# A graph attention stack on one core: the last all-node block of layers 2 and 3 holds three row tiles, and row tile 24 is gathered

## The chip, the core and the metric

The kernel runs on one core of a Trainium2 chip. The metric is device time in microseconds of that core, from start to end of one execution. A profiled execution gives the trace; the timed runs are separate executions without a profile.

## The reference

Four graph attention layers work on the same 4096 nodes with 256 features each. `adj` is a 4096 x 4096 0/1 matrix with a density of about 1/256 and ones on the diagonal. Each layer computes attention weights between every node and its neighbours, a softmax over the neighbours, the weighted sum of the projected neighbours, a residual and a layer norm:

```python
e = leaky_relu(s1[:, None] + s2[None, :], 0.2)        # per head
att = softmax(where(adj > 0, e, -huge), axis=1)
x = layernorm(x + att @ h)                            # h = x @ W, per head
```

Layers 0 and 1 have four heads of 64, layer 2 has two heads of 128. Layer 3 has one head of 256, computes the softmax of e and of -e, passes both weighted sums through one matrix and an ELU, and then does the same residual and norm.

## The kernel before, in words

Nodes are cut into 32 tiles of 128. A layer has two ways to compute a row tile (128 output nodes).

**Gathered.** Because the graph is sparse, layer 0 also builds lists of the neighbours of each row tile. `RowTile.load` (L781) fetches their projected values from HBM: one plain load of the tile's own rows and 13 indirect transfers `G<-vals,idx` of 128 rows each (L797), issued by POOL one after another. They come in two halves of seven places: half 0 has six gathers and reads only nodes of tiles under `MIX` = 23 (L85, L798); half 1 has seven and may read any node. `RowTile.half` (L835) then computes weights on ScalarE (`w`, L907 in layer 2, L874 in layer 3), masks them on VectorE (L909, L876, L878) and multiplies on TensorE (L928). The mask bits are spread to bytes at L660. The buffers `G` are four slots per half; a half takes one slot in layer 2 and two in layer 3, so in layer 3 POOL can be two tiles ahead.

**All-node.** `whole_rows` (L1168) computes a block of four row tiles against all 32 node tiles, without gathers. One unit is one node tile j: SyncE loads `vw` (L1188), VectorE spreads mask bits (L660), ScalarE computes weights `pw` for 512 columns (L1200, or L1203 with L1205 or L1207), VectorE masks them (L1201 or L1208), TensorE does four matmuls for each head (L1211). Layer 2's units do both heads (32 units a block); layer 3's do one of its two sums (64 units a block). All TensorE inputs are fp32; the trace has two records for each matmul. `WHOLE` (L115) names the blocks of each layer: block 7 in layer 1, blocks 3, 7, 6 in layer 2, blocks 7, 6 in layer 3. `ORDER` (L117) is the rest, in rising order: layer 2 gathers 20 tiles (0 to 11, 16 to 23), layer 3 gathers 24 (0 to 23).

**Order of the work.** Each engine runs its instructions in the order in which the program was built. `half_with_whole` (L1046) is one half step: the half of a gathered tile, the projection of a finished tile into the next layer's values (transposes L677, copy L682, matmuls L691, exponent L711, product L725, store `vals<-row` L728), then the norm of the gathered tile before (L1360), then some units. `whole` (L995) paces the units evenly, so that they are used up six half steps before the layer's end; the block's tiles are finished after that (in layer 3 one per half step, through `zw`, L1376). A finished tile is projected two half steps later, tiles under `MIX` first (L1051). In `close` (L1106) what is left is projected, and the next layer's first loads and ten units are put in (`AHEAD`). Layer norms are done in groups of tiles (`GROUPS`, L82)[...].

So layer 3's first gathers on POOL wait for the values of all tiles under 23, and its half-1 gathers for all 32. POOL issues in program order: all of layer 2's gathers come before layer 3's first.

Of the kernel before, what the change touches and what calls it, by code (L numbers as in the profile page):

```python
# [37 lines left out]
F32 = mybir.dt.float32  # L38
# [3 lines left out]
I32 = mybir.dt.int32  # L42
I8 = mybir.dt.int8
U8 = mybir.dt.uint8
AF = mybir.ActivationFunctionType
# [5 lines left out]
P = 128  # L51
N = 4096
F = 256
NT = N // P
KT = F // P
BT = 4
# [22 lines left out]
UNITS = (1 + FIRST, NPACK - FIRST)  # L79
FULL = ((0,), tuple(range(NPAIR - FIRST, NPACK - FIRST)))  # L80
PAIRS = (tuple(range(1, 1 + FIRST)), tuple(range(NPAIR - FIRST)))
GROUPS = (((24, 4),), ((24, 2), (28, 1), (31, 2)), ((16, 2), (17, 1), (20, 2), (24, 1), (31, 2)), ((24, 1), (31, 4)))  # L82
LEAD = 4
LATE = 4
MIX = 23  # L85
# [26 lines left out]

WHOLE = ((), (7,), (3, 7, 6), (7, 6))  # L115
AHEAD = 10
ORDER = tuple([m for m in range(NT) if m // BT not in w] for w in WHOLE)  # L117

LEAST = 2.0611536224385579e-09

# [63 lines left out]
class Program:  # L184
# [99 lines left out]
    def lists(self, ctx):  # L284


        tc, nc, ins, shared = self.tc, self.nc, self.ins, self.shared
# [91 lines left out]
        class Block:  # L379
# [21 lines left out]
            def squeeze(self, part):  # L401
                js = slice(part * JG, (part + 1) * JG)
                src = self.mk.rearrange("p j t c -> p (j t c)").bitcast(I32) \
                    .rearrange("p (j t c) -> p j t c", j=JG, t=BT)
                w = P // 4
                for k in (4, 2, 1):
                    w //= 2
                    dst = self.bits[:, js] if k == 1 else wk.tile([P, JG, BT, w], I32, name=f"fold{k}", bufs=1)
                    nc.vector.scalar_tensor_tensor(dst, src[:, :, :, w:], k, src[:, :, :, :w],
                                                   op0=ALU.logical_shift_left, op1=ALU.bitwise_or)  # L410
                    src = dst
                if part == BT - 1:
                    rows = shared["v"][0][self.blk % 2][:N, :BW].rearrange("(j p) w -> p j w", p=P)
                    nc.sync.dma_start(out=rows, in_=self.bits.rearrange("p j t w -> p j (t w)").bitcast(F32))
                    if any(self.blk in w for w in WHOLE):
                        nc.sync.dma_start(out=shared["bitsW"][self.blk], in_=self.bits)

            def sort(self):
# [111 lines left out]
        prog, blocks = self, {}  # L530
# [424 lines left out]
class Layer:  # L955
# [212 lines left out]
    def whole_rows(self):  # L1168
        n, nc, prog, sh = self.n, self.nc, self.prog, self.shared
        H, Wd, T = HEADS[n], WIDTH[n], TERMS[n]  # L1170
        groups = [range(H)] if n < 3 else [(0,), (1,)]
        for blk in WHOLE[n]:
            tiles = range(blk * BT, (blk + 1) * BT)
            S = prog.bk.tile([P, T, BT, P], F32, name="Sw")
            for it, m in enumerate(tiles):
                nc.sync.dma_start(out=S[:, :, it, :], in_=sh["e"][n][m].partition_broadcast(P))
            bits = self.block_bits(blk)
            zs = [None] * BT
            for heads in groups:
                accs = [prog.bank(prog.pfour) for _ in range(BT)]  # L1180
                c0, c1 = heads[0] * Wd, (heads[-1] + 1) * Wd
                vs = {}

                def fetch(j):
                    if j >= NT:
                        return
                    vs[j] = prog.vp.tile([P, c1 - c0], F32, name="vw")
                    nc.sync.dma_start(out=vs[j], in_=sh["v"][n][0][j * P:(j + 1) * P, c0:c1])  # L1188

                for j in range(4):  # L1190
                    fetch(j)
                for j in range(NT):
                    fetch(j + 4)
                    mj = self.bytes(bits, j)
                    v = vs.pop(j)
                    for h in heads:
                        p = prog.dp.tile([P, BT, P], F32, name="pw")
                        d = sh["d"][n][:, j, h if n < 3 else 0:h + 1 if n < 3 else 1]
                        if n < 3:
                            nc.scalar.activation(p, S[:, h], AF.Exp, bias=d)  # L1200
                            nc.vector.scalar_tensor_tensor(p, p, LEAST, mj, op0=ALU.max, op1=ALU.mult)  # L1201
                        else:
                            nc.scalar.activation(p, S[:, 0], AF.Relu, bias=d)  # L1203
                            if h == 0:
                                nc.scalar.activation(p, p, AF.Exp, bias=sh["shift2"])  # L1205
                            else:
                                nc.scalar.activation(p, p, AF.Exp, scale=-1.0)  # L1207
                            nc.vector.tensor_tensor(p, p, mj, op=ALU.mult)  # L1208
                        c = h * Wd - c0
                        for it in range(BT):  # L1210
                            nc.tensor.matmul(accs[it][:, c:c + Wd], p[:, it, :], v[:, c:c + Wd],  # L1211
                                             start=(j == 0 and h == heads[0]), stop=(j == NT - 1),
                                             skip_group_check=True)
# [12 lines left out]

    def whole_heads(self):
# [7 lines left out]
        for blk in WHOLE[n]:  # L1235
            tiles = range(blk * BT, (blk + 1) * BT)
            S = prog.bk.tile([P, T, BT, P], F32, name="Sw")
# [10 lines left out]
            bits = self.block_bits(blk)  # L1248
            z = prog.bk.tile([P, BT, H, Wd], F32, name="zh")
            for up, flat in TWOS:  # L1250
                bu, bf = prog.bank(prog.pwhole), prog.bank(prog.pwhole)
                vs = {}
# [9 lines left out]
                for j in range(NT):  # L1262
                    fetch(j + 4)
                    mj = self.bytes(bits, j)
                    v = vs.pop(j)
                    p = {}
                    for h in (up, flat):
                        p[h] = prog.dp.tile([P, BT, P], F32, name="pw")
                        nc.vector.scalar_tensor_tensor(p[h], S[:, h], c[:, j, h:h + 1], mj, op0=ALU.max, op1=ALU.mult)  # L1269
                    how = dict(stop=j == NT - 1, skip_group_check=True)  # L1270
                    for it in range(BT):
# [5 lines left out]
                nc.scalar.copy(z[:, :, up, :], bu[:, :BT * Wd].rearrange("p (t c) -> p t c", t=BT))  # L1277
                turned = prog.bk.tile([Wd, BT, P], F32, name="turned")
                nc.scalar.copy(turned, bf[:Wd, :].rearrange("p (t i) -> p t i", t=BT))
                self.set_banks()  # L1280
                bt = prog.bank(prog.banks)
                for it in range(BT):
                    nc.tensor.transpose(bt[:, it * Wd:(it + 1) * Wd], turned[:, it, :], sh["ident"][:Wd, :Wd])
                nc.scalar.copy(z[:, :, flat, :], bt[:, :BT * Wd].rearrange("p (t c) -> p t c", t=BT))
# [12 lines left out]

    def load_x(self, m):
        y = self.prog.ld.tile([P, F], F32, name="y", bufs=13)
# [545 lines left out]
```

## Time and profile before

| what | value |
|---|---|
| median of 3 timed runs | 2787.8 us (2785.93 to 2805.77) |
| the profiled execution's own time | 2012.93 us |
| its span | 2011.1 us |
| TensorE clock granted, mean | 0.936 |
| PE, PEld, DVE, ACT, POOL busy | 1796.4, 1481.6, 1551.8, 1498.1, 1391.5 us |
| HBM traffic over the span | 224 GB/s |
| gathers `G<-vals,idx` | 1352, of 1025 ns mean |
| L1200 and L1203, 512 columns | 711 and 709 ns |
| L1201 and L1208, 512 columns | 686 and 689 ns |
| L909, 512 and 640 columns | 684 and 817 ns |
| L877, 512 and 640 columns | 715 and 821 ns |

The timed runs are 775 us longer than the profiled execution. All durations here are from that execution. Layer 2's last gather starts at 1489.8 us after the span's start, layer 3's first at 1533.2 and its last at 1978.4.

PE's busy time is modelled and its single durations overlap. What a matmul costs is better read from the chain of waits, where runs of records of one line stand with the time they took together. A gap of 0.3 us named "issue" stands between one gather and the next on POOL.

### The profile page before, as it was taken

How to read it: one execution, taken by the hardware profiler on the slowest of the kernel's cores; microseconds unless marked ns; L12 is line 12 of the kernel's file. 1: busy time of each engine (PE TensorE's matmuls, PEld its weight loads, DVE VectorE, ACT ScalarE, POOL GpSimd, SP SyncE). 2: the span in 40 equal slices, each digit the busy share in tenths (PEclk: the TensorE clock that was granted, in tenths of full speed). 3: DMA queues.
4: the chain of work that ended last, by engine and by line, in shares of the span. 5: the costliest groups of instructions: out<-in, count | busy, mean ns of one | idle time of the engine just before them, and what ended most of it. 6: DMA issues, size and time to landing. Idle time of an engine off the chain costs nothing.

```text
span 2011.1 us, 46792 instructions
## 1 busy us (share of the span) xinstructions
PE 1796.4 (89%) x15281; PEld 1481.6 (74%) x15281; DVE 1551.8 (77%) x5095; ACT 1498.1 (74%) x4659; POOL 1391.5 (69%) x1387
## 2 busy tenths in 40 slices
PE   5758889988999699998998989999998899899995
PEld 3537777777778589887886788898886677577773
DVE  3458988888889599988887877888876576676765
ACT  4559999898878577877666788877774687676863
POOL 0067777777777777777777677777753777767772
PEclk7758999999899799999999999999999999999998
DMA  8799999989767766666656656667666888888883
GB/s 292 227 336 325 319 298 286 293 293 296 217 170 203 200 177 190 180 182 178 179 167 183 194 158 189 199 189 203 184 187 188 248 266 247 266 251 251 258 250 105
DMA packets 291947, 453.59 MB, mean 226 GB/s; under 512 B 90246, under 2 KB 206059, under 8 KB 291692
## 3 DMA queue, kind: packets, MB, share of 16 engines
q0 software_dynamic: 74880, 227.83, 38.7%
q1 hardware_dynamic: 212194, 218.46, 35.0%
q10 hardware_dynamic: 4618, 4.20, 0.6%
q8 instruction: 123, 2.02, 0.4%
q14 instruction: 132, 1.08, 0.2%
HBM read 401.51 MB, written 48.81 MB: 224 GB/s over the span
## 4 chain that ended last, share of the span: by engine, by line
PE 46%; DMA 14%; ACT 12%; POOL 10%; DVE 9%; issue 6%; SPq 1%; DVEq 0%; ACTq 0%; POOLq 0%
PE bank L928 22%; PE bank L1211 12%; POOL G L797 10%; DMA G<-vals,idx 8%; ACT w L907 7%; PE bank L691 5%; DVE w L864 3%; DMA raw<-in_adjB_dram 2%; PE bank L1274 2%; ACT mk L399 1%; ACT pw L1200 1%; PE bank L1272 1%; DMA G<-vals 1%; PE bank L522 1%; PE bank L524 1%
## 5 line engine op out<-in xcount | busy, mean ns | idle before, releaser
L797 POOL DMA_INDIRECT G<-vals,idx x1352 | 1386.0, 1025 | 587.9 <-issue 350.0
L928 PE MATMUL bank<-G,w 128*64 128x130 f32 (+5 forms) x9156 | 920.8, 304 | 72.7 <-DVE w L864 60.7
L907 ACT ACTIVATE w<-S,G 128x64 f32<-128x64 f32 (+1 forms) x3080 | 824.3, 351 | 125.3 <-DMA G<-vals,idx 116.2
L928 PEld LDWEIGHTS bank<-G,w 128*64 128x64 f32 (+1 forms) x9156 | 741.4, 156 | 232.1 <-DVE w L864 76.5
L1211 PE MATMUL bank<-vw,pw 128*128 128x129 f32 (+1 forms) x2560 | 419.4, 322 | 13.7 <-issue 6.3
L1211 PEld LDWEIGHTS bank<-vw,pw 128*128 128x128 f32 x2560 | 375.1, 194 | 53.8 <-issue 17.7
L864 DVE SCALAR_TENSOR_TENSOR w<-w,bank 128x1024 f32<-128x1024 f32 (+1 forms) x240 | 322.7, 1345 | 10.2 <-ACT w L907 8.7
L691 PE MATMUL bank<-wext,xT 128*128 128x268 f32 (+3 forms) x640 | 185.6, 424 | 16.2 <-ACT xT L682 14.9
L874 ACT ACTIVATE w<-S,G 128x64 f32<-128x64 f32 (+1 forms) x329 | 104.1, 352 | 72.1 <-DMA G<-vals,idx 48.7
L691 PEld LDWEIGHTS bank<-wext,xT 128*128 128x128 f32 x640 | 121.4, 207 | 40.8 <-ACT xT L682 17.7
L1200 ACT ACTIVATE pw<-Sw,d 128x512 f32<-128x512 f32 x192 | 134.3, 711 | 21.0 <-PE bank L1211 12.5
L1201 DVE SCALAR_TENSOR_TENSOR pw<-pw,mw 128x512 f32<-128x512 f32 x192 | 129.5, 686 | 26.2 <-ACT pw L1200 25.1
L399 ACT ACTIVATE mk<-raw 128x1024 uint8<-128x1024 int32 x128 | 129.6, 1049 | 21.1 <-DMA raw<-in_adjB_dram 21.0
L1208 DVE TENSOR_TENSOR pw<-pw,mw 128x512 f32<-128x512 f32 x128 | 87.9, 689 | 63.1 <-ACT pw L1205 38.3
L903 DVE TENSOR_TENSOR w<-S,G 128x384 f32<-128x384 f32 x180 | 91.1, 509 | 41.8 <-DMA G<-vals,idx 36.2
L1203 ACT ACTIVATE pw<-Sw,d 128x512 f32<-128x512 f32 x128 | 89.7, 709 | 27.2 <-PE bank L928 10.4
L1272 PE MATMUL bank<-vw,pw 128*128 128x65 f32 x512 | 89.7, 258 | 17.5 <-DVE pw L1269 17.5
L1274 PE MATMUL bank<-pw,vw 128*65 128x128 f32 x512 | 99.7, 278 | 0.0
L1272 PEld LDWEIGHTS bank<-vw,pw 128*128 128x128 f32 x512 | 78.7, 195 | 26.2 <-issue 24.8
L1269 DVE SCALAR_TENSOR_TENSOR pw<-Sw,cw,mw 128x512 f32<-128x512 f32 x128 | 92.8, 740 | 0.0
L682 ACT COPY xT<-bank 128x256 f32<-128x256 f32 x128 | 45.7, 359 | 58.2 <-PE bank L677 37.9
L660 DVE TENSOR_TENSOR mw<-bw,pat 128x128 int32<-128x128 int32 x288 | 80.6, 285 | 1.6
(197 smaller groups left out, 1893.6 us busy)
## 6 DMA issues: line engine op xcount, KB each, us to landing
raw<-in_adjB_dram SPq DMA_DIRECT2D x128, 512.0 KB
G<-vals,idx POOLq DMA_INDIRECT x1352
vw<-vals SPq DMA_DIRECT2D x128, 128.5 KB
S<-edge SPq DMA_DIRECT2D x60, 256.0 KB
vw<-vals SPq DMA_DIRECT2D x96, 129.0 KB
xp<-y SPq DMA_DIRECT2D x96, 128.0 KB
y<-xp SPq DMA_DIRECT2D x96, 128.0 KB
vals<-row SPq DMA_DIRECT2D x64, 152.0 KB
```

What stands on the lines that cost most here:

```text
L399: nc.scalar.activation(self.mk[:, 2 * q:2 * q + 2], src, AF.Copy)
L691: nc.tensor.matmul(pp[:, :c1 - c0], self.xT[:, k, :], wext[:, k, c0:c1], start=(k == 0), stop=(k == KT - 1 and brow is None))
L797: nc.gpsimd.indirect_dma_start(out=self.row(half, k), out_offset=None, in_=self.values[:N + 1 if half else MIX * P, :].rearrange("r (k c) ...
L864: return nc.vector.scalar_tensor_tensor(pair, pair, LEAST, mh2, op0=ALU.max, op1=ALU.mult)
L874: nc.scalar.activation(w[0][:, u, rows], S[:, 0, rows], AF.Relu, bias=d(g, 0))
L907: nc.scalar.activation(w[h][:, u, rows], S[:, h, rows], AF.Exp, bias=d(g, h))
L928: nc.tensor.matmul(a, w[h][:, u, rows], b, start=half == 0 and u == 0 and (n == 3 or h == turns[0][0]), stop=half == 1, skip_group_check=True)
L1200: nc.scalar.activation(p, S[:, h], AF.Exp, bias=d)
L1201: nc.vector.scalar_tensor_tensor(p, p, LEAST, mj, op0=ALU.max, op1=ALU.mult)
L1211: nc.tensor.matmul(accs[it][:, c:c + Wd], p[:, it, :], v[:, c:c + Wd], start=(j == 0 and h == heads[0]), stop=(j == NT - 1), skip_group_ch ...
L1272: nc.tensor.matmul(bu[:, it * Wd:(it + 1) * Wd], p[up][:, it, :], v[:, up * Wd:(up + 1) * Wd], start=j == 0 and it == 0, **how)
L1274: nc.tensor.matmul(bf[:Wd, it * P:(it + 1) * P], v[:, flat * Wd:(flat + 1) * Wd], p[flat][:, it, :], start=j == 0 and it == 0, **how)
```

## The change

A block of `WHOLE` is now a range of row tiles that may be shorter than four. The last block of layers 2 and 3 becomes tiles 25 to 27 in place of 24 to 27. Tile 24 joins the gathered tiles as the last of `ORDER` (21 in layer 2, 25 in layer 3). The block's weights, masks and products are computed for three tiles: 384 columns in place of 512, three matmuls in place of four. Node values are loaded as before. The groups of norms follow. Layer 1's block 7 is the same as before. The diff, without layer 1's function and other places where only a 4 becomes a `g`:

```diff
-GROUPS = (((24, 4),), ((24, 2), (28, 1), (31, 2)), ((16, 2), (17, 1), (20, 2), (24, 1), (31, 2)), ((24, 1), (31, 4)))
+GROUPS = (((24, 4),), ((24, 2), (28, 1), (31, 2)), ((16, 2), (17, 1), (20, 2), (25, 1), (31, 2)), ((25, 1), (28, 3), (31, 4)))

...
-WHOLE = ((), (7,), (3, 7, 6), (7, 6))
+WHOLE = (
+    (),
+    (range(28, 32),),
+    (range(12, 16), range(28, 32), range(25, 28),),
+    (range(28, 32), range(25, 28),),
+)
-ORDER = tuple([m for m in range(NT) if m // BT not in w] for w in WHOLE)
+ORDER = tuple([m for m in range(NT) if not any(m in g for g in w)] for w in WHOLE)

...
         groups = [range(H)] if n < 3 else [(0,), (1,)]
-        for blk in WHOLE[n]:
-            tiles = range(blk * BT, (blk + 1) * BT)
+        for tiles in WHOLE[n]:
+            g = len(tiles)
             S = prog.bk.tile([P, T, BT, P], F32, name="Sw")
             for it, m in enumerate(tiles):
                 nc.sync.dma_start(out=S[:, :, it, :], in_=sh["e"][n][m].partition_broadcast(P))
-            bits = self.block_bits(blk)
-            zs = [None] * BT
+            bits = self.block_bits(tiles)
+            zs = [None] * g
             for heads in groups:
-                accs = [prog.bank(prog.pfour) for _ in range(BT)]
+                accs = [prog.bank(prog.pfour) for _ in range(g)]
                 c0, c1 = heads[0] * Wd, (heads[-1] + 1) * Wd
                 vs = {}
...
                     for h in heads:
-                        p = prog.dp.tile([P, BT, P], F32, name="pw")
+                        p = prog.dp.tile([P, BT, P], F32, name="pw")[:, :g]
                         d = sh["d"][n][:, j, h if n < 3 else 0:h + 1 if n < 3 else 1]
                         if n < 3:
-                            nc.scalar.activation(p, S[:, h], AF.Exp, bias=d)
+                            nc.scalar.activation(p, S[:, h, :g], AF.Exp, bias=d)
                             nc.vector.scalar_tensor_tensor(p, p, LEAST, mj, op0=ALU.max, op1=ALU.mult)
                         else:
-                            nc.scalar.activation(p, S[:, 0], AF.Relu, bias=d)
+                            nc.scalar.activation(p, S[:, 0, :g], AF.Relu, bias=d)
                             if h == 0:
                                 nc.scalar.activation(p, p, AF.Exp, bias=sh["shift2"])
                             else:
                                 nc.scalar.activation(p, p, AF.Exp, scale=-1.0)
                             nc.vector.tensor_tensor(p, p, mj, op=ALU.mult)
                         c = h * Wd - c0
-                        for it in range(BT):
+                        for it in range(g):
                             nc.tensor.matmul(accs[it][:, c:c + Wd], p[:, it, :], v[:, c:c + Wd],
                                              start=(j == 0 and h == heads[0]), stop=(j == NT - 1),
                                              skip_group_check=True)
                     if n == 3 and heads[0] == 0 and j == NT - 1:
                         def between(accs=accs):
-                            for it in range(BT):
+                            for it in range(g):
                                 zs[it], last = self.positive(accs[it], whole=True)
                             return last
                         self.between = between
...
-    def block_bits(self, blk):
+    def block_bits(self, tiles):
+        blk, t = divmod(tiles[0], BT)
         bits = self.prog.mwp.tile([P, NT, BT, MW], I32, name="bw")
         self.nc.sync.dma_start(out=bits, in_=self.shared["bitsW"][blk])
-        return bits
+        return bits[:, :, t:t + len(tiles)]
     def bytes(self, bits, j):
-        mj = self.prog.mup.tile([P, BT, P // 4], I32, name="mw")
+        g = bits.shape[2]
+        mj = self.prog.mup.tile([P, BT, P // 4], I32, name="mw")[:, :g]
         spread(self.nc, mj, bits[:, j], self.shared["pat"])
-        return mj.rearrange("p t i -> p (t i)").bitcast(U8).rearrange("p (t i) -> p t i", t=BT)
+        return mj.rearrange("p t i -> p (t i)").bitcast(U8).rearrange("p (t i) -> p t i", t=g)
```

More of the change, by code (lines that the diff above doesn't have):

```diff
@@ L414, in squeeze @@
                     nc.sync.dma_start(out=rows, in_=self.bits.rearrange("p j t w -> p j (t w)").bitcast(F32))
-                    if any(self.blk in w for w in WHOLE):
+                    if any(g[0] // BT == self.blk for w in WHOLE for g in w):
                         nc.sync.dma_start(out=shared["bitsW"][self.blk], in_=self.bits)
@@ L1234, in whole_heads @@
         nc.vector.tensor_scalar(c, c, HUGE, TINY, op0=ALU.min, op1=ALU.max)
-        for blk in WHOLE[n]:
-            tiles = range(blk * BT, (blk + 1) * BT)
-            S = prog.bk.tile([P, T, BT, P], F32, name="Sw")
+        for tiles in WHOLE[n]:
+            g = len(tiles)
+            S = prog.bk.tile([P, T, BT, P], F32, name="Sw")[:, :, :g]
             for it, m in enumerate(tiles):
@@ L1247, in whole_heads @@
                 nc.vector.tensor_scalar(S[:, h], S[:, h], LEAST, HUGE, op0=ALU.mult, op1=ALU.min)
-            bits = self.block_bits(blk)
-            z = prog.bk.tile([P, BT, H, Wd], F32, name="zh")
+            bits = self.block_bits(tiles)
+            z = prog.bk.tile([P, BT, H, Wd], F32, name="zh")[:, :g]
             for up, flat in TWOS:
@@ L1267, in whole_heads @@
                     for h in (up, flat):
-                        p[h] = prog.dp.tile([P, BT, P], F32, name="pw")
+                        p[h] = prog.dp.tile([P, BT, P], F32, name="pw")[:, :g]
                         nc.vector.scalar_tensor_tensor(p[h], S[:, h], c[:, j, h:h + 1], mj, op0=ALU.max, op1=ALU.mult)
                     how = dict(stop=j == NT - 1, skip_group_check=True)
-                    for it in range(BT):
+                    for it in range(g):
                         nc.tensor.matmul(bu[:, it * Wd:(it + 1) * Wd], p[up][:, it, :],
@@ L1276, in whole_heads @@
                     yield
-                nc.scalar.copy(z[:, :, up, :], bu[:, :BT * Wd].rearrange("p (t c) -> p t c", t=BT))
-                turned = prog.bk.tile([Wd, BT, P], F32, name="turned")
-                nc.scalar.copy(turned, bf[:Wd, :].rearrange("p (t i) -> p t i", t=BT))
+                nc.scalar.copy(z[:, :, up, :], bu[:, :g * Wd].rearrange("p (t c) -> p t c", t=g))
+                turned = prog.bk.tile([Wd, BT, P], F32, name="turned")[:, :g]
+                nc.scalar.copy(turned, bf[:Wd, :g * P].rearrange("p (t i) -> p t i", t=g))
                 self.set_banks()
                 bt = prog.bank(prog.banks)
-                for it in range(BT):
+                for it in range(g):
                     nc.tensor.transpose(bt[:, it * Wd:(it + 1) * Wd], turned[:, it, :], sh["ident"][:Wd, :Wd])
-                nc.scalar.copy(z[:, :, flat, :], bt[:, :BT * Wd].rearrange("p (t c) -> p t c", t=BT))
+                nc.scalar.copy(z[:, :, flat, :], bt[:, :g * Wd].rearrange("p (t c) -> p t c", t=g))
             for it, m in enumerate(tiles):
                 self.finish(m, z[:, it].rearrange("p h c -> p (h c)"), self.load_x(m), None)
-    def block_bits(self, blk):
+    def block_bits(self, tiles):
+        blk, t = divmod(tiles[0], BT)
         bits = self.prog.mwp.tile([P, NT, BT, MW], I32, name="bw")
         self.nc.sync.dma_start(out=bits, in_=self.shared["bitsW"][blk])
-        return bits
+        return bits[:, :, t:t + len(tiles)]
     def bytes(self, bits, j):
-        mj = self.prog.mup.tile([P, BT, P // 4], I32, name="mw")
+        g = bits.shape[2]
+        mj = self.prog.mup.tile([P, BT, P // 4], I32, name="mw")[:, :g]
         spread(self.nc, mj, bits[:, j], self.shared["pat"])
-        return mj.rearrange("p t i -> p (t i)").bitcast(U8).rearrange("p (t i) -> p t i", t=BT)
+        return mj.rearrange("p t i -> p (t i)").bitcast(U8).rearrange("p (t i) -> p t i", t=g)
     def load_x(self, m):
```

## The prediction

> **What bounds the kernel now.** I read the page's busy table first (PE 89%, POOL 69%), then cut the span at layer borders, because an average over four layers with different limits says little. The change touches layers 2 and 3 alone, so I asked for busy time in five stretches: layer 2's stream of gathers, the handover, the start of layer 3, its steady part, its tail. The columns are PE, PEld, DVE, ACT, POOL, clock, DMA share, GB/s.
>
> ```profile
> 1156.30:1491.00 334.70, 309.79 (x2697) 288.27 (x2696) 272.19 (x888) 267.21 (x772) 263.05 (x236) 0.96 0.66 189
> 1491.00:1533.20 42.20, 40.27 (x269) 32.09 (x267) 36.19 (x188) 20.24 (x57) 0.00 (x0) 1.00 0.43 135
> 1533.20:1600.00 66.80, 55.43 (x265) 41.62 (x266) 31.81 (x99) 40.64 (x88) 50.84 (x50) 0.90 0.81 241
> 1600.00:1953.00 353.00, 345.07 (x1866) 255.87 (x1865) 253.78 (x925) 265.43 (x601) 253.57 (x244) 0.99 0.84 258
> 1953.00:2011.00 58.00, 36.91 (x218) 25.41 (x216) 32.61 (x141) 19.66 (x51) 19.73 (x21) 0.86 0.41 119
> ```
>
> POOL looks loose (263 of 335 us) but is not: its waits show 0.3 us of "issue" before nearly every gather. In layer 2 it issues 236 gathers in 334.7 us, 1.42 us each, without one wait for a buffer. In layer 3 a gather costs 1.03+0.30 = about 1.34 us. Waits of POOL from 1530 us on:
>
> ```profile
> POOL G L797 <- issue: 76.1, 244, 2.0
> POOL G L797 <- ACT row L711: 42.2, 1, 42.2
> POOL G L797 <- PE bank L928: 23.9, 24, 5.6
> POOL G L797 <- ACT w L874: 9.6, 12, 2.2
> ```
>
> The 42.2 us is the handover: POOL has issued layer 2's last gather at 1489.8 and starts layer 3's first at 1533.2, when the values of row tiles under 23 are in HBM. "L928" and "L874" are PE and ACT holding gather buffers: in layer 3 POOL is held back. The chain of waits shows PE's period there, back to back (start, us, records):
>
> ```profile
> 1846.52 3.97 PE bank L928 x28
> 1850.48 5.40 PE bank L1211 x24
> 1855.88 4.68 PE bank L928 x28
> 1860.56 3.47 PE bank L1211 x16
> ```
>
> So a gathered tile costs PE 3.97+4.68 = 8.65 us in layer 3, and an all-node record (L1211) 5.20/24 = 0.217 us. In layer 2 the same chain gives 2.12+2.57 = 4.69 us a tile and 5.36/48 = 0.112 us a record. Layer 2 is close to a tie of PE and POOL; layer 3 is PE's, with POOL and DMA (0.84) close behind.
>
> **What the Trainium skill says.** "DMA: Bandwidth & Descriptors", section "SWDGE vs HWDGE vs iDMA": a gather's descriptors are computed by software on GpSimd. The trace agrees: 1.25 us from gather to gather at the least, one after another. The same page, "Issuing engines are not separate DMA queues": POOL's and SP's transfers share 16 engines, so more gathers press on the vw loads too (0.84 busy above). "TensorE: Matmul & The Clock Gate", "What's actually happening": the clock halves after an idle window. Agrees: at layer 3's start the 28 records took 5.84 and 7.62 us after waits of 5.84 and 5.40.
>
> **The change part by part**, in us of the profiled execution (2012.93, span 2011.1).
>
> 1. PE. Layer 2's last block: 32 units x 2 heads = 64 matmuls fewer, 2 records each: 128 x 0.112 = -14.3; tile 24 gathered +4.7; net -9.6. Layer 3: 128 x 0.217 = -27.7, +8.65; net -19.1. Together -28.7.
> 2. POOL: 13 gathers more in each layer: 13 x 1.42 = +18.4 and 13 x 1.34 = +17.4.
> 3. DMA. The vw loads stay (32 node tiles for three row tiles as for four). Added in layer 3: 14 tiles of 258 KB, 3.6 MB, 14 us at the 258 GB/s of the steady part. One edge load moves from Sw to S, one bits load of 28 KB comes in each layer; 5 and 4 us of SP's queue at most (0.32 us an issue), which waits for data far longer; I take nothing.
> 4. ACT and DVE. 384 columns were never run; from 512 and 640 wide (DVE 684 and 817 ns, ACT 711 and 821) a quarter less saves 0.13 and 0.11 us, bounds 0 and a quarter (0.17). Layer 2: DVE 64 x 0.13 = -8.5, gathered tile +4.3 (four masks 3.0, six small spreads 1.3); ACT -7.0, gathered (20 x 0.335 + 8 x 0.389) +9.8. Layer 3: DVE -8.5 +4.3, ACT 128 x 0.11 = -14, +7.8. Neither engine is the bound (75% busy in layer 3's steady part): nothing on the path; without PE as cover some 5 us either way.
> 5. Layer 2's end. Tile 24 is now the last gathered tile. Its gathers go into the 42 us hole: POOL ends near 1489.8+18.4 = 1508, data 3.8 us later (the last landing before), then ACT 2.3, mask 0.8, matmuls 2.6: 1518 at the least. Before, the last L928 of layer 2 ended at 1520.7, because PE lagged; PE now has 9.6 less to do, so it is no later than now. What is late next is layer 3's first gather. It needs tiles under 23 only. Tile 22's projection used to come one place later than the first L691 after the last half; by the compiled order of PE it is now that first one, whose value store SP issued at 1523.8 (tile 22's: 1529.5, landed 3.7 later). So the first gather moves to about 1519.3+3.1+3.7 = 1526, -7. The bound from the other side: 0, if DVE's small operations delay it.
> 6. Layer 3's stream. Before: 1533.2 to 1979.4 = 446.2, of which 312 x 1.34 = 418 are issue and 28 are waits for buffers. After, 118 units (ten go ahead) spread over 44 half steps: 54 of the full block at 1.73 us, 64 at 1.30. PE's period per tile: 8.65 + 5.36 x 1.73 = 17.9 in the first block, 15.6 in the second, against POOL's 13 x 1.34 = 17.4 (18.4 for PE before). So POOL waits only in the first block, 10 tiles x 0.5 = 5, and 6 at the bank change and the start: 11 in place of 28, -17. This is where PE's gain goes: POOL becomes the bound in the second block. Stream: -7 + 17.4 - 17 = -6.6.
> 7. The tail after the last gather (31.6 us) holds four all-node finishes on DVE; one fewer, 2.9 us of listed operations: -3.
>
> Sum -9.6, say -10: 2003. The timed runs take 2787.8, 775 more than the profiled execution, and no view shows where. If that is spread evenly, -10 becomes -14; if it lies elsewhere, it stays -10. I take -12: **2776**.
>
> **The rivals.**
> A, PE pays everywhere: the longer runs are longer because PE is slower, so PE bounds layers 2 and 3 throughout. -28.7 x 2787.8/2012.93 = -40: 2748. For: PE 98% busy in the steady part. Against: POOL's period of 17.4 lies only 1 us under PE's.
> B, slower: the gather stream is the bound. Place: POOL in layer 3. The 28 us of waits stay (with DMA near full, data comes later and buffers are freed later), and the first gather does not move: +17.4, 2805; if a gather takes 1.385 times as long in the timed runs and layer 2's 13 are not hidden either, +50: 2838. It decides from the point where a tile's gathers take longer than PE's period, 17.9. For: 17.4 is close. Against: in layer 0 POOL kept its 1.25 us at a DMA share of 0.94.
> C, nothing moves: the handover hides layer 2's gathers, layer 3's two sides cancel: 2788.
>
> **How the numbers follow.** Mine 0.45 (own range 2760 to 2788: the ends of steps 5 and 6), A 0.22, B 0.18, C 0.15. One per cent is 28 us, about what a measurement of this kernel can tell from no change. Faster by over 1%: A and a little of mine, 0.27. Slower: B's upper part, 0.14. The rest 0.59. The range reaches from A's far side, 2742, to B's nearer end, 2810.
>
> **What would show it.** Right: first layer 3 gather some 7 us earlier against layer 2's start; 325 gathers in layer 3 with under 15 us of waits on L928 and L874 together; ACT's waits for G longer in the second block; PE's busy share in the steady part lower. Wrong: POOL still waiting as long for PE (A), or DMA share over 0.95 with gathers over 1.4 us (B). Step 5 fails if the hole stays 42 us; step 7 if four zw operations still stand in the tail.

## The result, and the profile after

The changed kernel took 2811.95 us (median of 18 runs) against 2794.32 us for the kernel before (18 runs beside it): ratio 1.0062, interval 1.0043 to 1.0082, or 17 us more. The forecast was 2776 us.

One thing has to be known to read the rest. The runs of this study fell on different chips, and the kernel before took 2013 to 2015 us on some and 2744 to 2794 us on others, in every run of the chip. By their times, the profile that the prediction read was of the first kind, and the timed runs shown with it of the second; on which chips these ran is not on record. I call the two kinds chips A and chips B. Each chip was used at one time only, so whether the difference belongs to the chip or to the time isn't shown. Each ratio below was formed on one chip, against runs of the kernel before on the same chip.

On a chip A the same changed kernel took 1.0007 (0.9992 to 1.0022) of the time of the kernel before, where the forecast for the profiled execution was 0.995. Its profile there can be laid beside the one of before. First the busy time in the same five stretches: layer 2's stream, the handover, the start of layer 3, its steady part, its tail (PE, PEld, DVE, ACT, POOL, clock, DMA share, GB/s):

```profile
1157.80:1506.50 348.70, 310.29 (x2663) 285.01 (x2662) 271.94 (x935) 268.55 (x805) 272.50 (x251) 0.95 0.69 191
1506.50:1541.00 34.50, 31.90 (x207) 25.42 (x206) 24.51 (x133) 16.58 (x44) 0.02 (x2) 0.95 0.34 112
1541.00:1607.80 66.80, 56.09 (x265) 41.38 (x265) 33.96 (x103) 38.87 (x85) 51.02 (x46) 0.90 0.80 237
1607.80:1959.00 351.20, 340.28 (x1857) 248.39 (x1857) 257.12 (x977) 265.58 (x627) 267.80 (x260) 0.99 0.87 272
1959.00:2017.20 58.20, 30.80 (x180) 19.48 (x176) 30.56 (x131) 19.98 (x53) 21.00 (x22) 0.79 0.42 124
```

Layer 2's stream is 14 us longer (348.7 against 334.7) although PE has fewer matmuls; the handover is 7.7 us shorter (34.5 against 42.2). Both together end later than before. In the steady part PE is busy 5 us less, POOL 14 us more. POOL's waits from 1530 us on, in the same execution (the lines of the changed kernel's file stand five lower: L802, L879, L933 and L1216 are the L797, L874, L928 and L1211 of before; in the kernels of the experiments they can stand up to eight lower):

```profile
POOL G L802 <- issue: 74.9, 243, 1.1
POOL G L802 <- PE bank L696: 34.5, 1, 34.5
POOL G L802 <- PE bank L933: 8.5, 21, 1.5
...
POOL G L802 <- ACT w L879: 5.2, 12, 1.2
```

The first line is the 0.3 us between gathers. The waits for PE and ACT to free gather buffers fell from 23.9 and 9.6 to 8.5 and 5.2 us. The chain of waits in the second block no longer runs on PE alone: a transfer of node values stands between PE's pieces, where before they stood back to back.

```profile
1832.77 2.85 PE bank L1216 x12
...
1836.62 5.88 DMA vw<-vals
...
1842.63 2.84 PE bank L1216 x12
1845.47 4.68 PE bank L933 x28
```

On a chip B the trace of the changed kernel looks different. POOL's waits in layer 3 there:

```profile
POOL G L802 <- issue: 89.5, 273, 2.8
POOL G L802 <- PE bank L696: 46.7, 1, 46.7
POOL G L802 <- PE bank L933: 19.4, 13, 3.6
POOL G L802 <- ACT w L879: 17.0, 9, 3.1
```

POOL still waits for buffers. And TensorE pauses with nothing shown that it waits for, mostly in runs of gathered matmuls, as in this piece of PE's timeline in layer 0 (start, us; the wait before each in brackets):

```profile
576.76 0.45 PE L933 MATMUL bank<-G,w 128*64 128x130 f32 x1 [1.12 <-issue]
578.90 0.37 PE L933 MATMUL bank<-G,w 128*64 128x130 f32 x1 [1.69 <-issue]
581.01 0.37 PE L933 MATMUL bank<-G,w 128*128 128x130 f32 x1 [1.74 <-issue]
```

Over the whole span these pauses come to 504 us in 575 places, where the chip A trace has two. They are not the whole difference, for PE's busy time differs too, with the same number of records and a lower granted clock (0.82 against 0.93 as a mean). The chip B trace first, then the chip A trace:

```profile
PE 2102.6 (75%) x15137; PEld 1662.9 (60%) x15137; DVE 1550.7 (56%) x5130; ACT 1508.9 (54%) x4705; POOL 1392.2 (50%) x1413
```

```profile
PE 1774.7 (88%) x15137; PEld 1456.5 (72%) x15137; DVE 1543.5 (77%) x5130; ACT 1495.1 (74%) x4705; POOL 1419.0 (70%) x1413
```

The two traces of the changed kernel differ by 772 us, about the 775 that the prediction could not place: 597 lie in layers 0 and 1, which the change doesn't touch, 120 in layer 2 and the handover, 56 in layer 3.

### The profile page after: what moved, and what is told of

Read it like the earlier page. It is cut to its first block, busy times and chain, and to the rows that moved or that the text cites. A ratio compares the mean times of both kernels' runs of the same rounds, so it can differ in the third digit from the quotient of the medians.

```text
span 2789.7 us, 46645 instructions
## 1 busy us (share of the span) xinstructions
PE 2102.6 (75%) x15137; PEld 1662.9 (60%) x15137; DVE 1550.7 (56%) x5130; ACT 1508.9 (54%) x4705; POOL 1392.2 (50%) x1413
## 4 chain that ended last, share of the span: by engine, by line
PE 49%; issue 13%; ACT 4%; POOL 3%; DMA 2%; DVE 2%; another core or an unknown queue 1%; SPq 0%; ACTq 0%; POOLq 0%; DVEq 0%
PE bank L933 26%; PE bank L1216 12%; PE bank L696 4%; ACT w L912 3%; POOL G L802 3%; PE bank L1279 2%; PE bank L1277 2%; DMA G<-vals,idx 1%; PE bank L682 1%; PE bank L699 1%; DVE w L869 0%; ACT pw L1205 0%; PE bank L527 0%; PE bank L529 0%
## 5 line engine op out<-in xcount | busy, mean ns | idle before, releaser
L802 POOL DMA_INDIRECT G<-vals,idx x1378 | 1386.9, 1006 | 1365.2 <-issue 651.9
L933 PE MATMUL bank<-G,w 128*64 128x130 f32 (+5 forms) x9268 | 1164.6, 329 | 393.7 <-issue 357.6
L933 PEld LDWEIGHTS bank<-G,w 128*64 128x64 f32 (+1 forms) x9268 | 895.4, 173 | 632.1 <-issue 526.3
L1216 PE MATMUL bank<-vw,pw 128*128 128x129 f32 (+1 forms) x2304 | 415.1, 333 | 77.1 <-issue 72.8
L1216 PEld LDWEIGHTS bank<-vw,pw 128*128 128x128 f32 x2304 | 357.5, 203 | 130.2 <-issue 100.6
L696 PE MATMUL bank<-wext,xT 128*128 128x268 f32 (+3 forms) x640 | 214.1, 472 | 38.8 <-ACT xT L687 24.5
L716 ACT ACTIVATE row<-bank 128x4 f32<-128x4 f32 (+1 forms) x128 | 21.6, 169 | 322.2 <-remote 106.6
L1205 ACT ACTIVATE pw<-Sw,d 128x512 f32<-128x512 f32 (+1 forms) x192 | 128.3, 679 | 119.9 <-remote 58.7
L1206 DVE SCALAR_TENSOR_TENSOR pw<-pw,mw 128x512 f32<-128x512 f32 (+1 forms) x192 | 122.1, 643 | 114.8 <-ACT pw L1205 86.6
L879 ACT ACTIVATE w<-S,G 128x64 f32<-128x64 f32 (+1 forms) x343 | 111.3, 354 | 101.3 <-DMA G<-vals,idx 58.4
L718 DVE COPY row<-bank 128x6 f32<-128x6 f32 (+2 forms) x128 | 20.0, 156 | 229.9 <-ACT row L716 202.3
L1213 DVE TENSOR_TENSOR pw<-pw,mw 128x512 f32<-128x512 f32 (+1 forms) x128 | 79.1, 621 | 68.7 <-ACT w L879 12.4
L1277 PE MATMUL bank<-vw,pw 128*128 128x65 f32 x512 | 102.9, 288 | 15.9 <-issue 15.7
L747 ACT ACTIVATE erow<-bank,shift 4x128 f32<-4x128 f32 (+1 forms) x96 | 33.5, 352 | 130.9 <-PE bank L737 77.9
L515 DVE TENSOR_TENSOR under<-bank,ranks 128x512 f16<-128x512 f32 x32 | 21.9, 685 | 139.9 <-remote 68.4
```

The lines of the kernel that those rows point to most:

```text
L696: nc.tensor.matmul(pp[:, :c1 - c0], self.xT[:, k, :], wext[:, k, c0:c1], start=(k == 0), stop=(k == KT - 1 and brow is None))
L802: nc.gpsimd.indirect_dma_start(out=self.row(half, k), out_offset=None, in_=self.values[:N + 1 if half else MIX * P, :].rearrange("r (k c) ...
L879: nc.scalar.activation(w[0][:, u, rows], S[:, 0, rows], AF.Relu, bias=d(g, 0))
L933: nc.tensor.matmul(a, w[h][:, u, rows], b, start=half == 0 and u == 0 and (n == 3 or h == turns[0][0]), stop=half == 1, skip_group_check=True)
L1205: nc.scalar.activation(p, S[:, h, :g], AF.Exp, bias=d)
```

## The experiments

**Each part alone, on a chip A.** Four kernels: the kernel before again, the change in layer 2 alone, in layer 3 alone, and the whole change. The two halves differ from the changed kernel in two lines each (of `GROUPS` and `WHOLE` the part that differs is shown):

```diff
 # layer 2 only
-GROUPS: ((25, 1), (28, 3), (31, 4))
+GROUPS: ((24, 1), (31, 4))
-    (range(28, 32), range(25, 28),),
+    (range(28, 32), range(24, 28),),
 # layer 3 only
-GROUPS: ((16, 2), (17, 1), (20, 2), (25, 1), (31, 2))
+GROUPS: ((16, 2), (17, 1), (20, 2), (24, 1), (31, 2))
-    (range(12, 16), range(28, 32), range(25, 28),),
+    (range(12, 16), range(28, 32), range(24, 28),),
```

> The kernel before, once more, for a trace in the state of the timed runs (near 2790 us) and as a measure of what equal kernels differ by. Every theory: ratio 1.00 within 0.5%. Theory T1 (the added gathers cost POOL and DMA time in layers 2 and 3): the trace shows layers 2 and 3 together about 17 us shorter than in the kernel after, layers 0 and 1 equal. Theory T2 (PE pauses of about a microsecond between matmuls, which the trace files under issue, make up the 775 us; the change moves only their number): PE's issue waits on L928 are some hundred us, and near none in the first profile.

> Tile 24 gathered in layer 2 only; layer 3 as before. T1: layer 2 hides its 13 gathers in the handover, so 0 to +4 us (2790 to 2798). T2: the gathered tile's 28 small matmuls replace 64 large ones, cost unclear: between -5 and +12 us. Rival T3 (layer 2's own end is later by the whole gather, 18 us): +15 to +20.

> Tile 24 gathered in layer 3 only; layer 2 as before. T1: most of the loss is here, +10 to +18 us. T3: near 0. T2: between -10 and +10.

> The changed kernel on the same chip as the two halves: +12 to +23 us by its first comparison (1.0062). All theories: the sum of the two halves within 6 us if the halves do not interact; less than the sum if the cover of the handover serves both.

Measured: before 0.9992 (0.9980 to 1.0003), layer 2 alone 1.0052 (1.0033 to 1.0070), layer 3 alone 0.9950 (0.9934 to 0.9965), the whole 1.0007 (0.9992 to 1.0022). So the whole change is nothing there because a loss of 10 us in layer 2 meets a gain of 10 us in layer 3. The prediction had both as gains. The expectations written from the first result (T1 above all, with the loss in layer 3) had them the wrong way round for this kind of chip.

**Why layer 2 loses.** The traces gave two suspects. One (theory P): POOL's issue of gathers sets layer 2's pace, and 13 more make its stream longer. The other (theory H): the handover. This is ScalarE's timeline there in the layer-2-only kernel:

```profile
1540.73 0.35 ACT L879 ACTIVATE w<-S,G 128x64 f32<-128x64 f32 x1 [2.48 <-DMA G<-vals,idx]
1540.99 0.71 ACT L1210 ACTIVATE pw<-pw,shift 128x512 f32<-128x512 f32 x1
1545.17 0.35 ACT L879 ACTIVATE w<-S,G 128x64 f32<-128x64 f32 x1 [3.48 <-DMA G<-vals,idx]
...
1546.04 0.35 ACT L687 COPY xT<-bank 128x256 f32<-128x256 f32 x1
```

The copy that tile 24's projection needs was ready at 1539.3, when PE's transposes ended, but stood behind two weight operations of layer 3 that waited for their first gathers. PE waited 7.1 us for it:

```profile
1546.44 3.81 PE L696 MATMUL bank<-wext,xT 128*128 128x256 f32 x8 [7.09 <-ACT xT L687]
```

In the kernel before, the last copy stands ahead of these. The experiments: the copy put ahead by an ordering edge (in the layer-2-only kernel and in the whole change); the kernel before with 13 gathers more in layer 2; and the layer-2-only kernel with tile 24's 13 gathers replaced by plain loads of other rows, issued by SyncE (it leaves out tile 24's neighbours, so the tile's output is not the right one; the rest of the work is there).

```diff
 # copy first
+                with self.prog.tc.issue_after(proj.copied.ins):
-                following.tile(0).half(0)
+                    following.tile(0).half(0)
 # spare gathers, after the loop in RowTile.load
+        if n == 2 and half == 1 and m in ORDER[2][2:15]:
+            nc.gpsimd.indirect_dma_start(out=self.row(1, 0), ...)   # a second time
 # plain loads, in that loop
+            if n == 2 and m == 24:
+                nc.sync.dma_start(out=self.row(half, k), in_=self.values[k * P:(k + 1) * P, :ROW[n]])
+                continue
```

> The change in layer 2 alone (measured at 1.0052 of before), with one edge more: ScalarE's copy xT of tile 24's projection stands ahead of layer 3's first weights. Theory P (VectorE, ScalarE and TensorE all follow POOL in layer 2; 13 more gathers lengthen its stream by about 10 us): the ratio stays 1.004 to 1.007, and layer 2's stream of gathers stays near 382 us. Theory H (what costs is the handover: the copy waited behind two weight operations for layer 3's first gathers, TensorE idle for 7.1 us, tile 24's values late): tile 24's store comes 6 us earlier, and the ratio falls to 1.003 or less.

> The kernel before, with 13 gathers more in layer 2: in 13 of its tiles the first gather of half 1 is issued a second time, into the same rows. TensorE, VectorE and ScalarE do the same work. Theory P: 13 issues of 1.38 us on POOL are 18 us, of which 10 to 18 show: ratio 1.005 to 1.009, layer 2's stream of gathers 382 to 390 us in place of 372. Theory H and the prediction's step 5 (the hole before layer 3's first gather takes them): within 3 us of before, 0.9985 to 1.0015.

> The change in layer 2 alone, but tile 24's 13 gathers in layer 2 are plain loads of other rows, issued by SyncE: the tile's output is not the reference's, all other work is the same, and POOL has the 236 gathers of before in layer 2. Theory P: the loss of 10 us goes, ratio 0.998 to 1.002 (below 1 if TensorE's saving of 9.6 us then shows), layer 2's stream near 370 us. Theory H: the copy still stands behind two weight operations, so the ratio stays 1.003 or more.

> The whole change (measured at 1.0007 of before) with the same edge as in the first of these runs: tile 24's copy xT ahead of layer 3's first weights. Theory P: 0.999 to 1.0025, as without the edge. Theory H: 0.997 or less, since layer 3's half-1 gathers and its all-node units start 6 us earlier.

These four fell on a chip B. Measured: copy first 0.9999 (0.9976 to 1.0022), spare gathers 1.0053 (1.0031 to 1.0074), plain loads 0.9980 (0.9961 to 1.0000), whole change with the copy first 1.0047 (1.0026 to 1.0068). The first lies in H's range and under P's, but it has no partner without the edge on that chip; the last lies above both ranges, and is not told apart from the 1.0062 without the edge. The third speaks against H there: the late copy is still in that kernel (PE waited 7.0 us for it), H had forecast 1.003 or more, and there is no loss. What is clear: 13 gathers alone cost layer 2 14.8 us, and the smaller block with plain loads in their place is worth 5.6 us (the interval reaches from 0 to 11).

The next kernels were to tell two theories of layer 3 on chips B apart. S: pauses of the engines hold POOL up there, so the 13 gathers cost their full price and PE's smaller load gives nothing back. Q: layer 3 gains on both kinds. They fell on another chip A: the kernel before, the two halves, and the kernel before with the 13 spare gathers in layer 3 in place of layer 2 (`n == 3`).

> The kernel before, unchanged, for a trace on the chip of this call. Ratio 0.998 to 1.002. If the chip is one on which it takes some 2790 us (2013 in the trace of the prediction), TensorE shows over 400 us of pauses named issue, most of them in layers 0 and 1, and layers 2 and 3 together take at most 200 of the 775 us.

> The change in layer 3 alone. Where before takes 2013 us it measured 0.995. Theory S (where before takes 2790 us, pauses of the engines and not TensorE's load hold POOL up in layer 3, so 13 gathers more are 17 us more and nothing comes back): 1.003 to 1.007 on such a chip. Theory Q (layer 3 gains on every chip as TensorE's load falls, and the loss on the other chip was all layer 2's): 0.993 to 0.997 on both.

> The change in layer 2 alone. Where before takes 2013 us it measured 1.0052. Theory S: 0.999 to 1.003 where before takes 2790 us, since there the same part with the copy ahead gave 0.9999. Theory Q: 1.008 to 1.014 there, so that both parts together give the 1.0062 measured.

> The kernel before, with 13 gathers more in layer 3 (the first gather of half 1 issued twice in 13 of its tiles, into the same rows). TensorE's work stays. Theory S, where before takes 2790 us: 13 x 1.34 = 17 us show nearly in full, 1.004 to 1.007. Where before takes 2013 us, TensorE is 100% busy in the steady part and POOL waits 30 us for it: 6 us or less show, 1.000 to 1.003. Theory Q: 1.003 or less on both.

Measured: before 1.0009 (0.9996 to 1.0022), layer 3 alone 0.9966 (0.9951 to 0.9981), layer 2 alone 1.0078 (1.0063 to 1.0092), spare gathers in layer 3 1.0047 (1.0031 to 1.0062). The last is above what I gave for a chip A: even where POOL waited 28 us for buffers, 13 gathers cost 9.4 us, so its waits hid only about half of their 17.4.

The copy-first kernel on a chip A, with layer 3 alone beside it:

> The change in layer 3 alone. Where before takes 2790 us: theory S (TensorE's saving is lost there, and 13 gathers more cost their 17 us in layer 3) 1.003 to 1.007; theory Q (layer 3 gains on every chip) 0.993 to 0.997. Where before takes 2013 us: 0.995 to 0.998, as measured.

> The change in layer 2 alone with tile 24's copy xT ahead of layer 3's first weights. Where before takes 2013 us, the change in layer 2 without this edge measured 1.0052 and 1.0078. Theory H (the late copy is the loss): 1.003 or less. Theory P (13 gathers more on POOL are): 1.004 to 1.007. Where before takes 2790 us: 0.998 to 1.002, as measured.

Measured: layer 3 alone 0.9948 (0.9929 to 0.9966), copy first 1.0054 (1.0033 to 1.0075). The trace shows why this doesn't settle H. ScalarE's timeline in the copy-first kernel:

```profile
1539.73 0.35 ACT L687 COPY xT<-bank 128x256 f32<-128x256 f32 x1
...
1545.05 0.35 ACT L879 ACTIVATE w<-S,G 128x64 f32<-128x64 f32 x1 [3.97 <-DMA G<-vals,idx]
...
1550.63 0.15 ACT L716 ACTIVATE row<-bank 128x2 f32<-128x2 f32 x1
```

The copy ran 6 us earlier, but the next step of the same projection on ScalarE, the exponent, now stood behind seven weight operations, and the store of tile 24's values was issued at 1551.76, after 1551.44 without the edge. The wait had moved by one operation. The edit did not do what it was for. P's range for this kernel was met and H's was not, but with the values as late as before this neither shows H nor rules it out on a chip A.

The spare gathers in layer 2 and layer 3 alone, once more:

> The kernel before with 13 gathers more in layer 2 (the first gather of half 1 issued twice in 13 tiles). Theory P: they are the whole of what layer 2's part costs where before takes 2013 us, 1.005 to 1.009 there, with layer 2's stream of gathers 10 to 18 us longer and first gather of layer 3 as much later; where before takes 2790 us, 1.003 to 1.0075 as measured. If the ratio is 1.002 or less where before takes 2013 us, P falls: then it is the moved tile's own work.

> The change in layer 3 alone. Where before takes 2790 us: theory S 1.003 to 1.007 (TensorE's saving is lost there, 13 gathers more cost 17 us in layer 3), theory Q 0.993 to 0.997. Where before takes 2013 us: 0.995 to 0.997, as measured twice and once more.

Measured: spare gathers in layer 2 1.0088 (1.0069 to 1.0107), layer 3 alone 0.9962 (0.9947 to 0.9976). That is 17.7 us for 13 gathers, 1.36 us each: the full price of an issue on POOL. The two stretches around layer 2's last gather in this kernel:

```profile
1158.00:1511.00 353.00, 318.31 (x2713) 294.67 (x2710) 273.22 (x897) 265.12 (x772) 276.35 (x250) 0.95 0.66 186
1511.00:1553.70 42.70, 40.46 (x271) 32.31 (x270) 36.44 (x187) 20.02 (x58) 0.05 (x1) 1.00 0.41 131
```

The hole is 42.7 us, as long as before, and 18 us later. Nothing went into it.

**Layer 3 on a chip B.** The last two kernels were layer 3 alone again and the plain loads again, this time on a chip B.

> The change in layer 3 alone. Where before takes 2790 us: theory S 1.003 to 1.007 (TensorE's saving is lost there, 13 gathers more cost 17 us in layer 3), theory Q 0.993 to 0.997. Where before takes 2013 us: 0.995 to 0.997, as measured.

> The change in layer 2 alone with tile 24's 13 gathers in layer 2 as plain loads of other rows on SyncE: the tile's output is not the reference's, the rest of the work is the same. Where before takes 2013 us: theory P (layer 2 follows POOL; TensorE's saving of 9.6 us has nothing to act on) 0.998 to 1.001; if TensorE held layer 2, as the prediction's step 5 had it, 0.995 to 0.997. Where before takes 2790 us: 0.996 to 1.000, as measured.

Measured: layer 3 alone 1.0061 (1.0038 to 1.0084), plain loads 0.9973 (0.9951 to 0.9994). The first is in S's range and outside Q's. So the same part of the change gains 7 to 10 us on four chips A and loses 16.7 us on a chip B. The stretch in which it happens runs from layer 3's first half-1 gather to its last gather. One line for each kernel; on chips A the kernel before, then layer 3 alone:

```profile
1551.70:1980.90 429.20, 415.83 (x2230) 307.87 (x2228) 291.33 (x1044) 309.99 (x698) 310.40 (x299) 0.98 0.83 252
```

```profile
1552.00:1972.40 420.40, 403.44 (x2198) 292.55 (x2198) 287.95 (x1075) 303.82 (x717) 320.37 (x312) 0.99 0.86 267
```

On that chip B the kernel with plain loads, whose layer 3 is that of before, then layer 3 alone:

```profile
2258.10:2714.60 456.50, 429.12 (x2239) 314.09 (x2239) 294.91 (x1049) 317.80 (x706) 311.14 (x299) 0.97 0.79 238
```

```profile
2244.00:2725.20 481.20, 425.86 (x2158) 299.01 (x2155) 289.40 (x1079) 307.54 (x719) 314.99 (x313) 0.94 0.77 233
```

On chips A the stretch is 9 us shorter with the change, and PE's busy time falls by 12. On the chip B it is 25 us longer (over all traces there, 481 us as a mean of three kernels with the change and 463 of four without: 18 longer), and PE's busy time falls by only 3 us although it runs 81 records fewer. The reason shows in PE's waits in layer 3, plain loads first, then layer 3 alone:

```profile
PE bank L1219 <- issue: 17.4, 16, 1.9
PE bank L936 <- issue: 11.8, 15, 1.7
PE bank L696 <- ACT xT L687: 7.0, 1, 7.0
```

```profile
PE bank L933 <- issue: 40.9, 36, 5.7
PE bank L1216 <- issue: 18.5, 19, 1.8
```

The pauses without a named cause went from 29 to 59 us (29.1 in the copy-first kernel, whose layer 3 is that of before; 43.4 and 46.5 in the two kernels with the whole change), and the granted clock fell from 0.97 to 0.94. On chips A layer 3 has at most one of these, of some 6 us. The clock weighs as well: the 0.06 missing from full clock are 29 of the 481 us in layer 3 alone, the 0.03 with plain loads 14 of the 456 us. So on a chip B PE had less to do and wasn't done sooner, and POOL's waits beyond the 0.3 us stayed (65 to 71 us in the three kernels with the change in layer 3, 54 to 66 in the four without).

Are the pauses chance? The kernel with plain loads left traces of two chips B, with 552 and 518 pauses of PE. Of these, 220 stand before the very same records, of 15209; pauses strewn at random would share some 19 (552 x 518 / 15209). So they hang in good part on places in the program. What there is at these places, no run tells.

## Why the prediction was wrong

Its sum was -9.6 us for the profiled execution and -12 for the timed runs. Measured: +1.4 on a chip A, +17 on a chip B. Two of its steps failed, one on each kind of chip. For the timed runs of the forecast, which were of kind B, it is step 6 with the carrying over; on chips A it is step 5.

**Step 5, layer 2's end, failed on chips A: layer 3's first gather 7 us earlier was forecast; it came 2.5 us later, and layer 2's part cost 10.5 and 15.7 us in its two timings.** The step let tile 24's gathers "go into the 42 us hole". It put the last gathered product 10 us after the last gather (1508 to 1518), and in any case no later than the 1520.7 of before: that one was late "because PE lagged", and PE has 9.6 us less to do. But the hole is no slack of POOL's. It is the drain behind the last gather: data, weights, products, norm, projections, with PE busy 40 of its 42 us. In all thirteen traces of chips A the last gathered product of layer 2 ended 29.3 to 31.3 us after the last gather started, with the smaller block, without it, and with the spare gathers. PE's saving lies before the drain (in the changed kernel the block's last matmul ended at 1501, the last gather started at 1505.5), and so doesn't shorten it. When the last gather moved, the product moved with it, from 1520.7 to 1534.8.

With the change in layer 2 alone (three traces, one with the copy first, against three of before, in the mean) the last gather came 9.9 us later after layer 2's first, and the hole was 7.4 us shorter, which makes the 2.5. The -7.4 is the one place that tile 22's projection moves up, which step 5 forecast as -7; what it missed is that the hole began 10 us later. The +9.9 is 13 x 1.25 = 16.3, the least price of the gathers, less some 5 us because the gathers of this layer ran shorter than before (their time over 0.95 us each fell from 44 to 39 us in sum), less a wait of 5 us in one of the traces of before; why they ran shorter, no run tells.

Two more losses have no term in the step. From layer 3's first gather to its first half-1 gather took 4.0 us longer, and the steady stretch after it 4.2. The first of the two is one instruction: the second gather of layer 3. The kernel before, then layer 2 alone:

```profile
1535.86 1.03 POOL L797 DMA_INDIRECT G<-vals,idx  x1 [0.30 <-issue]
```

```profile
1538.06 4.63 POOL L802 DMA_INDIRECT G<-vals,idx  x1 [0.31 <-PE bank L737]
```

It took 4.62 or 4.63 us in all nine traces with the smaller block in layer 2, on both kinds of chip, with and without the copy edge and with the plain loads, and 0.95 to 1.08 us in ten of the eleven others (2.42 in one). What held it isn't shown. As for the 4.2, in the compiled order only 28 of layer 3's all-node records ran ahead of its first gathered product, against 60 before. 32 x 0.217 = 7 us of PE's work then came later, in a layer that PE bounds. How much of this the late copy causes stays open, since the edge that was to free it only moved the wait.

On chips B this step looks right, by few traces: layer 3's first gather came 532 to 539 us after layer 2's first in the whole change and in the copy-first kernel, 540 in the one trace with layer 2 as before, and the copy-first kernel timed at 0.9999. The 17 us of the timed runs are the size of layer 3's part alone there, 16.7.

My own view of the waits had shown it: in layer 2 POOL had not one wait for a buffer. An engine that never waits sets the pace, and "close to a tie of PE and POOL" was the wrong reading. The sign that the prediction named for this step, "the hole stays 42 us", was the wrong sign too: the hole shrank and the step failed all the same.

**Step 6, layer 3's stream, held on chips A and failed on chips B.** On chips A the waits for buffers went to 5 us in layer 3 alone (11 forecast, 28 before), the stream fell from 447 to 438 us (-9; the forecast without step 5's -7 was 0), and transfers and POOL now stand in the second block's chain as forecast. Its two sizes were off the same way: the waits fell by 23 us in place of 17, and the 13 issues added 15 in place of 17.4. On chips B the -17 of this step did not come: PE's saving of 19 us went into pauses and a lower clock. In the mean POOL's waits rose by 7 us (three kernels against four), and its issues by 11. "TensorE: Matmul & The Clock Gate" of the Trainium skill, section "What's actually happening", has the clock halve after an idle window of about 3.4 us. Here it halved without one. In layer 3 alone on the chip B it did so eight times from 2429 us on, each time after 3.4 us in which PE was busy 0.6 to 1.6 us, with no single pause over 1.8 us. The first of them (the columns are as in the tables of stretches; the clock is the third number from the end):

```profile
2425.60:2429.00 3.40, 1.64 (x8) 0.77 (x8) 2.14 (x9) 0.85 (x2) 1.43 (x2) 1.00 0.72 199
2429.00:2432.40 3.40, 3.40 (x11) 2.18 (x8) 2.19 (x9) 3.40 (x10) 2.21 (x3) 0.50 0.64 184
```

So in this trace several short pauses cost clock, where the page speaks of an idle window.

**The carrying over to the timed runs failed.** "If that is spread evenly, -10 becomes -14; if it lies elsewhere, it stays -10" left out the third case, that the 775 us come from another bound. Some 504 us of TensorE's pauses stand in the trace of such a run. In layer 3 work taken from PE gave nothing back there; in layer 2, with plain loads, it gave 5.6 and 7.4 us.

**The smaller steps.** Step 1's savings of PE, 9.6 and 19.1 us, show on chips A as 9 and 17 in PE's busy time over the span; 12.4 of the 17 lie in the long stretch. Its 0.217 us is written as 5.20/24 under a line that says 5.40, which would be 0.225 (the last line shown, 3.47/16, gives 0.217), and the 1519.3 of step 5 stands in no view of the trace; neither is worth more than some 3 us. Step 2's price, 17.4 to 18.4 for 13 gathers, was right: 17.7 in layer 2. Step 3, DMA: its share rose from 0.83 to 0.86; transfers stand in the new chain, and what they cost was not separated. Step 4's sums held: over the span VectorE was busy 9 us less in the whole change (8.4 forecast), ScalarE 4 less (3.4). Step 7: three `zw` operations stand in the tail in place of four, but from the last gather to the end it is 0.9 us shorter in layer 3 alone and not shorter at all in the whole change, where -3 was forecast.

**The rivals.** B said 2805 us at the least and named the place and the size: the waits stay, the first gather does not move, 17.4 us in layer 3. That is what chips B show, in sum: 2811.95 is 17.6 us over the kernel before. Its cause is not what they show: DMA share is 0.77, not near full, and its point of decision, a tile's gathers longer than PE's period, was not reached, since in layer 3 alone a gathered tile took 19.9 us of the stream with 17.1 of issue. A, that PE pays everywhere, had the longer runs right as PE's and the conclusion wrong: PE was slow there because it paused and its clock was lower, not because it had more to do. C, nothing moves, gives the time of chips A, by a loss and a gain and not by cover.

Layer 3's part alone is the best kernel on chips A and 0.6% slower than before on the chip B tried; no kernel here beats the one before on both. What makes TensorE pause on a chip B, and why the smaller block raises the pauses in layer 3, stays open; only that they are there, in good part at fixed places of the program, and that the part loses with them, is shown.

## What to carry to other kernels

An idle stretch between two streams of one engine is cover only if nothing that ends it hangs on the stream before it: ask whether it moves when the stream grows. The engine without waits sets the pace, however close another one's load is. And if the timed runs are a third longer than the profiled execution, get a trace from where they ran before pricing anything: the bound there may be another.

## What was not expected of the hardware

The same kernel took 2013 to 2015 us on four chips and 2744 and 2789 us on two others. It is not that operations of ScalarE, VectorE or POOL are slower there: ScalarE's gathered weights took 353 ns as a mean against 352, VectorE's masks 621 against 623, a gather 1003 against 1028 (layer 3 alone on both kinds). What differs are pauses and TensorE's clock: in the changed kernel 504 us of TensorE's pauses, 106 of VectorE's and 129 of ScalarE's, where the trace of the other kind shows 3, 5 and 1, and a mean clock of 0.82 against 0.93, with which TensorE's records took 323 ns as a mean against 302. And the second gather of layer 3 took 4.63 us, in place of about 1, in every kernel with the smaller block in layer 2.
